# Projecting and norming queries, keys and values by time step in phase one, through DRAM, instead of by tile in phase two

## The chip, the cores and the metric

The kernel runs on one core of a Trainium2 chip. The core has five engines that each work through their own instructions in order: TensorE (PE; its weight loads are listed apart as PEld), VectorE (DVE), ScalarE (ACT), GpSimd (POOL) and SyncE (SP, which here only issues DMAs). They wait for each other through semaphores. The metric is the device time of one execution in microseconds, lower is better. The median of three runs before the change is 867.8 us (867.76 to 870.64).

## The reference, cut to what matters

The input `x` has 128 sequences of 32 time steps with 256 channels; `cond` has one vector of 256 per sequence.

```python
# layer 0: a recurrence over the 32 steps, started at q = p = cond, driven by x
for t in range(32):                                   # RK4: four derivatives a step
    q, p = rk4_step(q, p, x[:, t], coupling, bias)    # tanh(q) @ coupling.T, q**3, ...
    trace[:, t] = q
x = x + mx_ffn(trace, w_gate, w_up, w_down)           # block-quantized gated FFN, 256 -> 1024 -> 256

# layer 1: attention over the 32 steps of each sequence, modulated by cond
scale, shift = split(cond @ W_emb + b_emb)
xn = rms_norm(x, g_norm) * (1 + scale) + shift
q, k, v = split(xn @ W_qkv)                           # 256 -> 768, 16 heads of 16
q, k = rms_norm(q, g_q), rms_norm(k, g_k)             # over the 16 channels of each head
o = softmax(q @ k.T * 16 ** -0.5) @ v
y = o + o @ W_out
# a second FFN: Hadamard rotation, 8-bit activations, ternary weights, 256 -> 1024 -> 256
x = x + h_ffn(y, w1_gate, w1_up, w1_down)
```

Layer 0 walks in time with all 128 sequences in the partitions. The attention of layer 1 needs all 32 steps of a sequence.

## The kernel before

**Phase one** goes by time step: a tile is [128 sequences, 256 channels] of one step. `drive` transposes the step's input, `step` does the recurrence (four slopes, each a chain of tanh on ACT at L594, products with `coupling` on PE at L601, a cube on POOL at L608 and sums on DVE at L552; the new state is written at L645), and `ffn0` does the first FFN of the step: quantizing, DMA transposes (L434), gate and up products (L929), silu (L937), the product on DVE (L941), down products (L976), and the store of the sum to `x1_dram` (L984). `ffn0` ends with the modulated norm: a square sum (L988), an inverse root on POOL (L993, L994), and then gain and shift. For the steps before `T - LATE` the scaling is done on ACT (L999) and gain and shift on POOL (L1003, L1007); for the last `LATE` steps DVE does both (L1012, L1014). The result is transposed on PE (L1015) and copied by ACT (L1017) with a stride of 32 elements into one SBUF tile `xnT` [128, 2, 128 sequences, 32 steps], in which a sequence's steps lie side by side. In the first 78 us the quantizing of the first FFN's weights (`mx_weight`) runs beside the first steps of the recurrence; `ternary_weight` prepares those of the second towards the end of phase one.

**Phase two** (`tokens`) goes by 32 tiles of 128 tokens: 4 sequences with their 32 steps each. The first tile waits for all 32 copies into `xnT`. A tile multiplies its 128 columns of `xnT` with `W_qkv` (`qk` at L1125, `v` at L1132, into PSUM slots of `ps_one`). ACT copies the values into a pad of 17 columns per head whose last column is 1 (L1141) and squares queries and keys (L1142); DVE sums the squares per head (L1143). `rsqrt` takes the inverse root by integer arithmetic on DVE (L1091) and ten tiny instructions on POOL (L1099 to L1109), after one that scales (L1088). DVE then multiplies the queries (L1148) and the keys (L1155) from PSUM with it; the keys go into a zeroed pad (three buffers of `coupling` that phase one no longer needs, cleared at L1052; those for the values are filled at L1058). POOL multiplies the queries with the gains (L1160), DVE transposes queries and keys in 32x32 blocks (L1167, L1169). Small matmuls make the logits (L1177) and the weighted values (L1207); softmax, output rotation (L1230), quantizing, gate and up (L1263), three butterfly stages split over POOL and DVE (L1294), a PE transpose (L526, `turn`), the Hadamard products (L1305), the down products (L1328) and the store (L1338) follow.

**Order.** Nothing runs in the order of the source. Each `add(engine, cost, fn, reads, writes, ..., rank=...)` makes an item; `Work.order` plays a list scheduler with the written costs, forth and back up to 40 times, and keeps the order with the earliest end. Buffers are taken from pools of slots (`states` has 6, `mid` 10); an item that finds none free waits. `port=True` keeps such items of POOL and DVE apart in the plan. `keep_warm` puts matmuls of zeros (L1354) into planned gaps of PE. All items of phase one are issued before those of phase two on every engine, and PSUM is divided anew between them (`ps_gu`, `ps_turn` and others in phase one, `ps_one` and `ps_two` in phase two). All DMAs, transposes too, go through SP's queue.

Of the kernel before, what the change touches and what calls it, by code (L numbers as in the profile page):

```python
# [20 lines left out]
P = 128  # L21
# [12 lines left out]
HEADS = 16  # L34
# [154 lines left out]

# [133 lines left out]
def kernel(  # L323
# [45 lines left out]
    states = slots("states", N, 6)  # L369
# [9 lines left out]
    slim_8 = slots("slim_8", N, 2, FP8)  # L379
    phase_one = ExitStack()  # L380
# [88 lines left out]
    b_xnT, xnT = fixed("xnT", [P, NC, B, T])  # L469
    xnT_flat = xnT.rearrange("p c b t -> p c (b t)")  # L470
    x1_dram = dram.tile([B, T, N], F32, name="x1_dram")
    x1_flat = x1_dram.rearrange("b t d -> (b t) d")
    out_flat = out.rearrange("b t d -> (b t) d")
# [87 lines left out]
    started, xnT_done, x1_stored = [], [], []  # L561
# [317 lines left out]
    LATE = 5  # L879
# [14 lines left out]
    def ffn0(t, q):  # L894
# [115 lines left out]
        else:  # L1010
# [5 lines left out]
        xnT_done.append(  # L1016
            add(ACT, 0.4, lambda: nc.scalar.copy(xnT[:, :, :, t], two(px.ap)), [px], fills=[b_xnT], rank=rank)  # L1017
        )

    q = Buf(())  # L1020
    q.slots, q.slot, q.writers = b_condT.slots, 0, b_condT.writers
    p = b_p
    weights_rank = -300.0
    TERNARY = 24
    parts = ((w0_gate, w0gT, b_w0g), (w0_up, w0uT, b_w0u), (w0_down, w0dT, b_w0d))
    for n, (w, dst, b_dst) in enumerate(parts):
        for part in range(2):
            mx_weight(w, dst, b_dst, part, weights_rank + 2 * n + part)
    modulation(-200.0)
    b_hf, had_ffn, b_qkv, w_qkv_sb = constants_of_phase_two(12.0)  # L1030
    d_next = drive(0, FIRST)
    for t in range(T):
        d = d_next
        if t + 1 < T:
            x_of[t + 1] = load_x(x_step, t + 1, t - 501.0)
            d_next = drive(t + 1, t - 499.9)
        q, p = step(t, q, p, d)
        ffn0(t, q)
    parts = ((w1_gate, w1gT, b_w1g), (w1_up, w1uT, b_w1u), (w1_down, w1dT, b_w1d))
    for n, (w, dst, b_dst) in enumerate(parts):  # L1040
        ternary_weight(w, dst, b_dst, n, T + n, started[TERNARY : TERNARY + 1])


    KPADS, VPADS = 3, 4
    PHASE_TWO = work.SECOND

    k_pads, v_pads = [], []
    pads_ready = []
    for b_c, c_mat in zip(b_coup[:KPADS], coup):
        k_pad = c_mat.rearrange("p c n -> p (c n)").rearrange("p (r a d) -> p r a d", a=4, d=D_HEAD)  # L1050
        pads_ready.append(
            add(POOL, 0.6, lambda k_pad=k_pad: nc.gpsimd.memset(k_pad, 0.0), [], [b_c], rank=float(T))  # L1052
        )
        k_pads.append(Slot(k_pad))

    for i in range(VPADS):
        v_pad = tile_of(f"v_pad{i}", [P, HEADS, D_HEAD + 1])
        nc.gpsimd.memset(v_pad, 1.0)  # L1058
        v_pads.append(Slot(v_pad))

    down_of = []
# [4 lines left out]
    def quantum(name, src, n, cost, rank):  # L1066

        am, sc = Buf(tiny), Buf(tiny)
        add(
            DVE, cost,  # L1070
            lambda: nc.vector.tensor_reduce(  # L1071
                am.ap[:, 0:1], src.ap[:, :n], AX.X, ALU.max, apply_absolute_value=True
            ),
            [src], [am], rank=rank,
        )

        def scales():
            nc.vector.tensor_scalar(am.ap[:, 0:1], am.ap[:, 0:1], EPS_QUANT, 1.0 / 127.0, ALU.max, MULT)
            nc.vector.reciprocal(sc.ap[:, 0:1], am.ap[:, 0:1])  # L1079

        add(DVE, 0.25, scales, [], [am, sc], rank=rank)
        return am, sc
# [30 lines left out]
    def tokens(g):  # L1113
        rank = PHASE_TWO + g
        tok = slice(g * P, (g + 1) * P)
        tt, ts = nc.vector.tensor_tensor, nc.vector.tensor_scalar
        first = list(xnT_done) if g == 0 else []
        behind = down_of[g - 7 : g - 6] if g >= 7 else []


        pqk, pv = Buf(ps_one), Buf(ps_one)

        def qk():
            for c in range(NC):
                nc.tensor.matmul(  # L1125
                    pqk.ap, lhsT=xnT_flat[:, c, tok], rhs=w_qkv_sb[:, c, : 2 * N],
                    start=(c == 0), stop=(c == NC - 1),
                )

        def v():  # L1130
            for c in range(NC):
                nc.tensor.matmul(  # L1132
                    pv.ap[:, :N], lhsT=xnT_flat[:, c, tok], rhs=w_qkv_sb[:, c, 2 * N :],
                    start=(c == 0), stop=(c == NC - 1),
                )

        add(PE, 1.72, qk, [b_xnT, b_qkv], [pqk], rank=rank, after=first, behind=behind)
        add(PE, 0.86, v, [b_xnT, b_qkv], [pv], rank=rank, after=first, behind=behind)
        v_pad, sq, qn, k_pad = Buf(v_pads), Buf(mid), Buf(slim), Buf(k_pads)
        sq_sum, rstd = Buf(tiny), Buf(tiny)  # L1140
        add(ACT, 0.26, lambda: nc.scalar.copy(v_pad.ap[:, :, :D_HEAD], heads(pv.ap[:, :N])), [pv], [v_pad], rank=rank)  # L1141
        add(ACT, 0.477, lambda: nc.scalar.activation(sq.ap, pqk.ap, AF.Square), [pqk], [sq], rank=rank)  # L1142
        add(DVE, 0.6, lambda: nc.vector.tensor_reduce(sq_sum.ap, heads(sq.ap), AX.X, ADD), [sq], [sq_sum], rank=rank)  # L1143

        rsqrt(sq_sum, rstd, 1.0 / D_HEAD, EPS_RMS, rank)
        add(
            DVE, 0.335,
            lambda: tt(heads(qn.ap), heads(pqk.ap)[:, :HEADS, :], spread(rstd.ap[:, :HEADS], D_HEAD), MULT),  # L1148
            [pqk, rstd], [qn], rank=rank,
        )  # L1150

        def k_mult():
            kv = heads(pqk.ap)[:, HEADS:, :].rearrange("p (r e) d -> p r e d", e=2)
            rk = rstd.ap[:, HEADS:].rearrange("p (r e) -> p r e", e=2)
            tt(k_pad.ap[:, :, 0::3, :], kv, rk.unsqueeze(3).to_broadcast([P, PAIRS, 2, D_HEAD]), MULT)  # L1155

        add(DVE, 0.335, k_mult, [pqk, rstd], [k_pad], rank=rank, after=pads_ready)
        add(
            POOL, 0.69,
            lambda: nc.gpsimd.tensor_tensor(  # L1160
                heads(qn.ap), heads(qn.ap), g_prod.unsqueeze(1).to_broadcast([P, HEADS, D_HEAD]), MULT
            ),
            [b_gp], [qn], rank=rank, port=True,
        )

        qT, kT, pl = Buf(slim), Buf(mid), Buf(ps_one)
        add(DVE, 0.335, lambda: nc.vector.transpose(qT.ap, qn.ap), [qn], [qT], rank=rank)  # L1167
        add(
            DVE, 0.63, lambda: nc.vector.transpose(kT.ap, k_pad.ap.rearrange("p r a d -> p (r a d)")),  # L1169
            [k_pad], [kT], rank=rank,  # L1170
        )
# [31 lines left out]
        def attend(group):  # L1203
            for hd in group:
                for j in range(BT):
                    row = slice(j * T, (j + 1) * T)
                    nc.tensor.matmul(  # L1207
                        by_v(po.ap)[row, hd, :], lhsT=by_head(exT.ap)[row, hd, :], rhs=v_pad.ap[row, hd, :],
                        start=True, stop=True,
                    )  # L1210

        for k in range(0, HEADS, HEADS // 2):
            add(
                PE, 0.63, lambda k=k: attend(range(k, k + HEADS // 2)), [exT, v_pad], fills=[po], rank=rank,
# [202 lines left out]
```

## Time and profile before

| | |
|---|---|
| median of 3 runs | 867.8 us |
| the profiled execution | 868.0 us |
| its span | 866.2 us |
| mean granted clock of PE | 0.986 |
| busy in the span: PE, PEld | 795.1 us (92%), 598.6 us (69%) |
| DVE, ACT, POOL | 732.2 us (85%), 494.0 us (57%), 615.9 us (71%) |
| moved by DMA | 55.53 MB, mean 64 GB/s |

The profile is one execution. An engine is busy while an instruction of its own runs; waits, branches and DMA issues are not counted. Matmuls are pipelined and their records overlap, so PE's busy share overstates its work; the distance between starts is the better measure. A line number is a line of the kernel; helpers such as `turn` (L526) and `load` (L444) have one line for many uses, and the names of the tiles tell them apart. "x8" is a count of instructions, and "[0.39 <-POOL slim L608]" is idle time before an instruction and what ended it.

### The profile page before, as it was taken

What the parts mean: (1) busy time and instruction counts of PE and PEld (TensorE: products, weight loads), DVE (VectorE), ACT (ScalarE), POOL (GpSimd) and SP (SyncE); (2) the same over time, 40 slices, a digit from 0 to 9 for tenths busy, and PEclk for the clock granted to TensorE, in tenths of its full rate; (3) what the DMA queues carried; (4) which work ended last, traced back from release to release, by engine and by line L of the source; (5) the groups of instructions that cost most, each with busy time, mean ns of one, the idle gap of its engine ahead of it and who ended that gap; (6) DMA issues with size and microseconds to landing.
All of it is one profiled execution on the core that took longest, in us unless ns stands there. A gap on an engine that the chain in (4) does not pass through costs nothing. (4 is left out here: it accounts for less than half of the span.)

```text
span 866.2 us, 26286 instructions
## 1 busy us (share of the span) xinstructions
PE 795.1 (92%) x10506; PEld 598.6 (69%) x10506; DVE 732.2 (85%) x1863; ACT 494.0 (57%) x1009; POOL 615.9 (71%) x955
## 2 busy tenths in 40 slices
PE   7789999999999999997789999999999999899986
PEld 4566778877788788775456667666667676576765
DVE  6889989999989999998677887778878788887694
ACT  3233465655466665754335667666767555776755
POOL 5698898888768888899574776656685676676320
PEclk9999999999999999999799999999999999999999
DMA  7222232313122242435500113221221221221334
GB/s 241 84 38 53 59 82 59 74 49 83 35 65 68 70 134 56 92 67 110 117 2 15 27 39 65 49 49 32 52 50 48 56 48 42 48 43 46 60 68 86
DMA packets 128891, 55.53 MB, mean 64 GB/s; under 512 B 102144, under 2 KB 127616, under 8 KB 128768
## 3 DMA queue, kind: packets, MB, share of 16 engines
q1 hardware_dynamic: 128768, 53.85, 26.9%
q8 instruction: 82, 1.34, 0.6%
q14 instruction: 41, 0.34, 0.1%
HBM read 21.32 MB, written 8.39 MB: 34 GB/s over the span
## 5 line engine op out<-in xcount | busy, mean ns | idle before, releaser
L1294 POOL TENSOR_TENSOR wide<-wide 128x512 f32<-128x512 f32 x116 | 149.1, 1306 | 68.7 <-DVE wide L1278 33.6
L601 PEld LDWEIGHTS ps_stage<-slim,coup 128*128 128x128 f32 x1024 | 129.3, 192 | 18.1 <-ACT slim L594 10.6
L601 PE MATMUL ps_stage<-slim,coup 128*128 128x128 f32 x1024 | 139.4, 279 | 0.6 <-ACT slim L594 0.3
L608 POOL TENSOR_TENSOR slim<-slim,slim 128x256 f32<-128x256 f32 x96 | 72.4, 755 | 27.7 <-ACT slim L595 23.0
L587 PE MATMUL ps_stage<-slim,eye 128*128 128x256 f32 x256 | 76.6, 392 | 8.1 <-DVE slim L552 7.8
L587 PE MATMUL ps_stage<-drives,eye 128*128 128x256 f32 x256 | 79.2, 392 | 3.3 <-DVE ps_stage L552 2.0
L956 POOL TENSOR_TENSOR mid<-mid,tiny 128x512 f32<-128x512 f32 x64 | 66.2, 1047 | 3.7 <-DVE tiny L678 3.2
L964 POOL TENSOR_TENSOR wide_bf<-mid,tiny 128x512 bf16<-128x512 fp8e4 x64 | 66.5, 1050 | 1.4 <-DVE mid L888 1.1
L594 ACT ACTIVATE slim<-slim 128x256 f32<-128x256 f32 x96 | 39.3, 409 | 47.4 <-DVE slim L552 44.6
L1305 PE MATMUL ps_two<-had_ffn,wide 128*128 128x128 f32 x512 | 63.3, 278 | 1.3 <-DVE wide L1278 1.2
L595 ACT ACTIVATE slim<-slim 128x256 f32<-128x256 f32 x96 | 39.2, 408 | 43.1 <-DVE slim L552 43.0
L1305 PEld LDWEIGHTS ps_two<-had_ffn,wide 128*128 128x128 f32 x512 | 59.9, 192 | 5.4 <-ACT wide L1300 1.9
L1125 PE MATMUL ps_one<-w_qkv_sb,xnT 128*128 128x512 f32 x128 | 60.7, 599 | 0.5 <-DVE mid L1196 0.2
L1313 ACT ACTIVATE wide<-ps_two,magic,tiny 128x1024 f32<-128x1024 f32 x32 | 38.5, 1203 | 39.5 <-DVE tiny L1079 28.0
L587 PEld LDWEIGHTS ps_stage<-slim,eye 128*128 128x128 f32 x256 | 42.0, 190 | 24.0 <-DVE slim L552 16.1
L1294 DVE TENSOR_TENSOR wide<-wide 128x512 f32<-128x512 f32 x76 | 53.3, 727 | 5.9 <-POOL wide L1294 5.9
L1278 DVE SCALAR_TENSOR_TENSOR wide<-ps_two,tiny,mid 128x512 f32<-128x512 f32 x64 | 46.4, 737 | 12.0 <-ACT mid L1271 11.3
L1207 PEld LDWEIGHTS ps_one<-v_pad,mid 32*32 32x32 f32 x4096 | 42.2, 106 | 20.8 <-issue 15.4
L1271 ACT ACTIVATE mid<-ps_two,tiny 128x512 f32<-128x512 f32 x64 | 43.0, 686 | 21.9 <-PE ps_two L1263 21.6
L1207 PE MATMUL ps_one<-v_pad,mid 32*32 32x17 f32 x4096 | 48.0, 181 | 4.5 <-issue 3.0
L587 PEld LDWEIGHTS ps_stage<-drives,eye 128*128 128x128 f32 x256 | 40.3, 193 | 12.3 <-DVE ps_stage L552 7.7
L1263 PEld LDWEIGHTS <-slim_bf 128*128 128x128 bf16 x256 | 24.0, 97 | 34.3 <-issue 8.3
(169 smaller groups left out, 2188.7 us busy)
## 6 DMA issues: line engine op xcount, KB each, us to landing
x_step<-in_x_dram SPq DMA_DIRECT2D x32, 128.0 KB, 2.1
x_add<-in_x_dram SPq DMA_DIRECT2D x32, 128.0 KB, 2.1
x_dram<-slim SPq DMA_DIRECT2D x32, 128.0 KB, 1.9
slim<-x_dram SPq DMA_DIRECT2D x32, 128.0 KB, 2.6
out_dram<-slim SPq DMA_DIRECT2D x32, 128.0 KB, 1.7
raws<-in_L_ffn_w_gate_dram SPq DMA_DIRECT2D x4, 512.0 KB, 4.8
raws<-in_L_ffn_w_up_dram SPq DMA_DIRECT2D x4, 512.0 KB, 6.3
raws<-in_L_ffn_w_down_dram SPq DMA_DIRECT2D x4, 512.0 KB, 4.0
```

What stands on the lines that cost most here:

```text
L587: PE, cost, lambda: nc.tensor.matmul(ps[i].ap, lhsT=eyes[eye], rhs=src.ap, start=False, stop=False),
L594: add(ACT, 0.32, lambda: nc.scalar.activation(th.ap, qi.ap, AF.Tanh), [qi], [th], rank=rank, table="silu")
L601: nc.tensor.matmul(ps[i].ap[:, sl], lhsT=coup[i][:, c, sl], rhs=two(th.ap)[:, c, :], start=False, stop=(c == NC - 1 and m == NC - 1),)
L608: POOL, 0.685, lambda: nc.gpsimd.tensor_tensor(sq.ap, sq.ap, qi.ap, MULT),
L956: lambda it=it, ks=ks: nc.gpsimd.tensor_tensor(blocks(it.ap), blocks(it.ap), spread(binv.ap[:, ks], BLOCK), MULT),
L964: lambda b8=b8, ks=ks, sl=sl: nc.gpsimd.tensor_tensor(blocks(bq.ap[:, sl]), blocks(b8.ap), spread(bscl.ap[:, ks], BLOCK), MULT),
L1125: nc.tensor.matmul(pqk.ap, lhsT=xnT_flat[:, c, tok], rhs=w_qkv_sb[:, c, : 2 * N], start=(c == 0), stop=(c == NC - 1),)
L1207: nc.tensor.matmul(by_v(po.ap)[row, hd, :], lhsT=by_head(exT.ap)[row, hd, :], rhs=v_pad.ap[row, hd, :], start=True, stop=True,)
L1271: lambda pgu=pgu, act=act: nc.scalar.activation(act.ap, pgu.ap[:, :HALF], AF.Silu, scale=sgu.ap[:, 0:1]),
L1278: lambda pgu=pgu, act=act, sl=sl: stt(it.ap[:, sl], pgu.ap[:, HALF:], sgu.ap[:, 1:2], act.ap, MULT, MULT),
L1294: eng.tensor_tensor(dv[:, :, e, :], sv[:, :, 0, :], sv[:, :, 1, :], op)
L1305: nc.tensor.matmul(pfh.ap[:, sl], lhsT=iT.ap[:, sl], rhs=had_ffn, start=True, stop=True)
```

## The change

The projection, the norm of queries and keys and the padding are taken out of the tiles of phase two and put at the end of every time step of phase one, in a function `token` that `ffn0` calls. There the partitions hold sequences. The step's queries, padded keys and padded values make one row of 256 + 512 + 272 = 1040 floats per sequence, which is stored to a DRAM tensor `tok_dram` [128, 32, 1040]. A tile of phase two loads its 128 rows from it into one of six slots; the first such load waits for all 32 stores. The transposed step goes to a small tile by a plain copy, and the large `xnT` is gone. ACT also copies queries and keys from PSUM to SBUF (`raw`), and DVE's two products read that copy. The pads of six slots are preset once. `rsqrt` is the same function, moved up. `LATE` goes from 5 to 14 and `states` from 6 to 8.

```diff
-    states = slots("states", N, 6)
+    states = slots("states", N, 8)
...
+    KEYS, VALUES, TOKEN = N, N + HALF, N + HALF + HEADS * (D_HEAD + 1)
+    toks = slots("tok", TOKEN, 6)
+    xns = slots("xns", N, 8)
...
-    b_xnT, xnT = fixed("xnT", [P, NC, B, T])
-    xnT_flat = xnT.rearrange("p c b t -> p c (b t)")
+    tok_dram = dram.tile([B, T, TOKEN], F32, name="tok_dram")
+    tok_flat = tok_dram.rearrange("b t d -> (b t) d")
...
-    LATE = 5
+    LATE = 14
...
         add(PE, 0.22, lambda: turn(px.ap, xn.ap), [xn], [px], rank=rank)
-        xnT_done.append(
-            add(ACT, 0.4, lambda: nc.scalar.copy(xnT[:, :, :, t], two(px.ap)), [px], fills=[b_xnT], rank=rank)
+        xnT = Buf(xns)
+        add(ACT, 0.26, lambda: nc.scalar.copy(xnT.ap, px.ap), [px], [xnT], rank=rank)
+        token(t, xnT)
+
+    toks_ready = []
+    for slot in toks:
+        def preset(ap=slot.ap):
+            nc.gpsimd.memset(ap[:, KEYS:VALUES], 0.0)
+            nc.gpsimd.memset(ap[:, VALUES:], 1.0)
+        toks_ready.append(add(POOL, 1.05, preset, rank=1.0))
...
+    def token(t, xnT):
+        rank = t + 0.4
+        tt = nc.vector.tensor_tensor
+        pqk, pv, raw, sq, tok = Buf(ps_gu), Buf(ps_turn), Buf(mid), Buf(mid), Buf(toks)
+        sq_sum, rstd = Buf(tiny), Buf(tiny)
...
+        add(PE, 1.72, qk, [xnT, b_qkv], [pqk], rank=rank)
+        add(PE, 0.86, v, [xnT, b_qkv], [pv], rank=rank)
+        add(
+            ACT, 0.26, lambda: nc.scalar.copy(values(tok.ap)[:, :, :D_HEAD], heads(pv.ap)), [pv], fills=[tok],
+            rank=rank, after=toks_ready,
+        )
+        add(ACT, 0.477, lambda: nc.scalar.activation(sq.ap, pqk.ap, AF.Square), [pqk], [sq], rank=rank)
+        add(ACT, 0.477, lambda: nc.scalar.copy(raw.ap, pqk.ap), [pqk], [raw], rank=rank)
+        add(
+            DVE, 0.6, lambda: nc.vector.tensor_reduce(sq_sum.ap, heads(sq.ap), AX.X, ADD), [sq], [sq_sum],
+            rank=rank,
+        )
+        rsqrt(sq_sum, rstd, 1.0 / D_HEAD, EPS_RMS, rank)
...
+        add(
+            DVE, 0.335,
+            lambda: tt(
+                heads(tok.ap[:, :KEYS]), heads(raw.ap)[:, :HEADS, :], spread(rstd.ap[:, :HEADS], D_HEAD), MULT
+            ),
+            [raw, rstd], fills=[tok], rank=rank, port=True, after=toks_ready,
+        )
+        add(DVE, 0.335, k_mult, [raw, rstd], fills=[tok], rank=rank, port=True, after=toks_ready)
+        tok_stored.append(
+            add(SP, 0.45, lambda: nc.sync.dma_start(tok_dram[:, t, :], tok.ap), [tok], rank=rank, tail=4.0)
+        )
...
     def tokens(g):
...
-        add(PE, 1.72, qk, [b_xnT, b_qkv], [pqk], rank=rank, after=first, behind=behind)
-        add(PE, 0.86, v, [b_xnT, b_qkv], [pv], rank=rank, after=first, behind=behind)
...
+        tok = Buf(toks)
+        add(
+            SP, 0.45, lambda: nc.sync.dma_start(tok.ap, tok_flat[rows, :]), fills=[tok], rank=rank, tail=4.0,
+            after=[*tok_stored, *toks_ready], behind=behind,
+        )
+        def gains():
+            q = heads(tok.ap[:, :KEYS])
+            nc.gpsimd.tensor_tensor(q, q, g_prod.unsqueeze(1).to_broadcast([P, HEADS, D_HEAD]), MULT)
+        add(POOL, 0.69, gains, [b_gp], [tok], rank=rank, port=True)
...
+        add(DVE, 0.335, lambda: nc.vector.transpose(qT.ap, tok.ap[:, :KEYS]), [tok], [qT], rank=rank)
+        add(DVE, 0.63, lambda: nc.vector.transpose(kT.ap, tok.ap[:, KEYS:VALUES]), [tok], [kT], rank=rank)
```

## The prediction

> **What bounds the kernel now.** I read the share of busy time first, then busy time by stage, then the order on single engines inside a stage, then the boundary of the phases. The profiled execution took 868.0 us: a span of 866.2 and 1.8 around it; the median of the runs is 867.8, so the sum below, made against 868.0, needs no scaling. About 0.5% (4.3 us) is what a measurement can tell from no change.
>
> Busy time by stage (columns: PE, PEld, DVE, ACT, POOL, each with its instruction count; then the granted clock, DMA share, GB/s). The cuts are at the first product of gate and up (77.6), the end of the last recurrence step (398), the end of the last copy into `xnT` (431) and the first transpose of phase two (439.7):
>
> ```profile
> 77.60:398.00 320.40, 314.13 (x2075) 249.49 (x2076) 302.29 (x859) 183.37 (x522) 274.22 (x362) 1.00 0.30 70
> 398.00:431.00 33.00, 22.26 (x122) 14.61 (x122) 25.81 (x56) 15.02 (x38) 24.15 (x31) 0.79 0.56 124
> 431.00:439.70 8.70, 8.28 (x27) 4.43 (x27) 3.57 (x8) 2.54 (x5) 3.72 (x14) 1.00 0.12 23
> 439.70:500.00 60.30, 53.37 (x1436) 36.23 (x1434) 48.42 (x117) 30.00 (x50) 38.92 (x105) 0.97 0.07 16
> 500.00:830.00 330.00, 307.83 (x6293) 227.45 (x6293) 264.46 (x642) 220.07 (x310) 213.96 (x381) 0.99 0.23 49
> 830.00:866.20 36.20, 26.84 (x212) 21.59 (x212) 24.49 (x49) 17.70 (x18) 2.95 (x2) 1.00 0.35 79
> ```
>
> In the body of phase one PE is busy 98%, DVE 94%, POOL 86%. In the body of phase two PE is busy 93%, DVE 80%, ACT 67%, POOL 65%. Matmul records overlap, so I checked on PE's timeline that 98% means full. Starts follow each other by 0.43 us, which is what two passes of 128x256 f32 take, without a gap:
>
> ```profile
> 208.28 0.60 PE L587 MATMUL ps_stage<-drives,eye 128*128 128x256 f32 x2
> 208.72 0.59 PE L587 MATMUL ps_stage<-slim,eye 128*128 128x256 f32 x2
> 209.15 0.59 PE L929 MATMUL ps_gu<-w0gT,slim_bf 128*128 128x512 bf16 x2
> 209.58 0.59 PE L587 MATMUL ps_stage<-slim,eye 128*128 128x256 f32 x2
> ```
>
> So PE is the bound in both phases, DVE is just behind it in phase one, and only DVE, ACT and POOL have room in phase two.
>
> At the boundary, one chain runs nearly alone:
>
> ```profile
> 430.35 0.59 ACT L1017 COPY xnT<-ps_turn 128x256 f32<-128x256 f32 x1 [3.22 <-PE ps_turn L526]
> 431.32 5.32 PE L1125 MATMUL ps_one<-w_qkv_sb,xnT 128*128 128x512 f32 x12
> 435.21 0.24 POOL L1099 TENSOR_TENSOR tiny<-tiny 128x32 f32<-128x32 f32 x1 [0.30 <-DVE tiny L1091]
> 438.09 0.25 POOL L1109 TENSOR_TENSOR tiny<-tiny,tiny 128x32 f32<-128x32 f32 x1
> 438.79 0.42 DVE L1155 TENSOR_TENSOR coup<-ps_one,tiny 128x256 f32<-128x256 f32 x1
> 439.72 0.70 DVE L1169 STREAM_TRANSPOSE mid<-coup 128x512 f32<-128x512 f32 x1
> ```
>
> **The change, part by part.** 32 tokens' worth of projection and norm move from phase two to phase one; the amount is the same, since there are 32 time steps and 32 tiles.
>
> *PE.* One tile's four passes at L1125 take 1.71 us and its four at L1132 0.86 (consecutive starts at 579.08, 580.79 in the chain that ended last), so 2.57 a tile, 82.2 us in all. Phase one after 77.6 lasts 353.4 us. PE's work there is 314.1 + 22.3 less the fillers of L1354 (0.9 + 6.8): 328.7, and 24.7 stay unfilled, mostly in the drain after the last recurrence step. With the same unfilled time phase one grows by the whole 82. From below: the drain takes half of the unfilled time, +70. From above it is POOL's turn.
>
> *POOL.* A token's inverse root is one instruction at L1088 (0.29) and ten from 435.21 to 438.34 (3.13): 3.42 us, 109.4 in all, while the planner books 0.24 + 2.4. Away go nine steps of gain and shift (0.727 + 0.742 each, 13.2 us; LATE from 5 to 14) and the clearing at L1052 (2.7). The presets of six slots (0.891 + 0.324 by L1052 and L1058, 7.3 us) fit in the 19.6 us that POOL idles before 77.6. POOL's work after 77.6 goes from 298.4 to 391.9. With its present 55 us of idle time that is 446.9 us, +93.5; at its present 84% it is 464, +111. I take PE's +82, because PE's work (410.9) is still the longer, and keep the others for the range.
>
> *DVE.* By distance of starts, L1143 costs 0.58, L1091 0.11, L1148 and L1155 0.34 each: 1.37 a token, 43.8 in all. Nine more steps of L1012 and L1014 (0.39 + 0.35) add 6.7. DVE after 77.6 goes from 328.1 to 378.6, below PE; it costs nothing beyond PE's 82 as long as that covers it. Without that cover its 50.5 us would meet its own 25.3 us of idle time there: 25 to 50 us.
>
> *ACT.* L1141 (0.37) and L1142 (0.59) move; the copy of queries and keys to `raw` is new and priced by L1142, 0.59. Added are 50 us, less 9 x 0.47 at L999 and about 0.24 a step for the plain copy in place of L1017's strided one. ACT goes from 198 to some 236 of 435: covered by PE. If PE's cover were gone ACT would still have 100 us free.
>
> *The two products now read two SBUF tiles* where L1148 and L1155 read one PSUM operand. Nearest rows: L1294 on DVE, two SBUF operands, 727 ns for 128x512, against 680 at L941 with one in PSUM, so 0.05 us longer at twice the size. I take 0.03 each, 64 of them, 2 us on DVE, not on the path; below nothing if the SBUF read is the shorter, as at L1014 (417 against 421 at L1148).
> The Trainium skill, page "SBUF — State Buffer", section "Who interferes with whom", says that a DVE instruction with two SBUF inputs contends with a GpSimd instruction that reads SBUF. If each of the 64 had to wait out half a POOL instruction (0.36 us by L1003), the sum by that rule, an estimate, is 23 us more on DVE and some of it on the path; the L1294 row shows a tenth of that, and the row decides.
>
> *Stores.* Each step adds a store of 128 rows of 4160 bytes, 520 KB, on SP behind DVE's product of the keys. Issue is 0.33 to 0.53 by the loads of 512 KB. Behind it in SP's queue stand the next x load, the x1 store and two DMA transposes a step (1.25 each): SP issues under 4 us in a step of 11, so there is cover. 32 stores are 17 MB; the 512 KB rows land in 4.0 to 6.3 us. Transfers run at 30% DMA share in phase one, and in 300 to 325, where three such loads pass, the transposes land in 2.6 and 3.2 us against 2.3 and 3.1 overall: up to 0.3 us a transposition, hidden in PE's queue. I take 0, up to 10 us for the phase. Phase two reads the 17 MB back at 23% share: also 0, while the loads run ahead over six slots.
>
> *The boundary.* The last token's chain from `xnT` to the products stays. Between the products and the first transpose come a store and a load that wait for every store before them. By the 128 KB rows (1.9 and 2.6, two issues 0.7) that is 5.2 us; by the 512 KB rows (4.0 and 6.3) 11. I take 4.5 + 4.5 + 0.7, less the 0.5 us that lies there now: +9, with all engines waiting. After it gain and transposes follow as before.
>
> *Phase two.* From 439.7 to the end are 426.5 us. PE's work without fillers is 388.0 - 12.4 = 375.6; of the moved 82.2 us 7.4 lay before 439.7, so 74.8 leave, to 300.8. DVE's work goes from 337.4 by 43.8 - 3.6 to 297.2: level with PE. With PE's unfilled time as now (50.9) the gain is 75; two close engines hinder each other, so I take 73. Bounds: 87, if the waits behind POOL's inverse root (17.3 us at L1148, 7.3 at L1155) held PE and half of the 25.7 us of its gaps in the body close; 40, if DVE keeps its 89 us of idle time. States from 6 to 8 and the dropped pads have no price of their own.
>
> Sum: +82 + 9 - 73 = +18: 868 + 18 = **886 us**.
>
> The skill's page "Perfetto Trace Analysis", section "Optimization Strategy", speaks against this forecast: where the most-contended engine changes over time, interleaving the regimes may help. Here the rows say that PE is the longest in both regimes, so PE's part moves from one full stage to another; only by the rule would the result be the first rival's time.
>
> **Rivals.** *The drain is filled and phase two runs freer* (faster): the tokens' products fill half of 398 to 431, the boundary costs 5, phase two gains 87: +70 + 5 - 87 = -12, 856. For it speak the 0.79 clock and 6.8 us of fillers in the drain, and the three PSUM tiles less per tile; against it, that the last token's chain is as long as before. It decides once phase two drops below 435 - 82 = 353 us and phase one grows by less than 75.
> *POOL sets phase one* (slower still): POOL is planned 0.8 us a token too short, every engine behind it waits in order; +100 + 11 - 73 = +38, 906. For: 86% busy already and +93 us. Against: LATE 14 takes 13 back.
> *The move does nothing for phase two*, since DVE is level: +82 + 9 - 55 = +36, 904.
> *No change*: all terms cancel within 4 us.
>
> **Chances.** Forecast 0.45; POOL or DVE 0.23 together; the drain rival 0.23; no change 0.09. Faster 0.23, same 0.09, slower 0.68. The range 857 to 914 reaches from the drain rival's time to a POOL case with phase one at +107; each end leaves out about 1 in 10. The likeliest case alone spans 873 to 898.
>
> **What would show it.** Right: in the body of phase one PE at 97% or more at 13.3 to 14 us a step, POOL near 90%, the last step's end at about 470, first transposes near 531, then 355 us; a gap of 8 to 10 us on all engines after the last store. Wrong: phase one longer by under 70 (then the drain took the work), or POOL without gaps while PE waits for L1109's successor (then POOL is the bound), or phase two above 370 with DVE over 90%, or transposes that land after 4 us and PE waiting for them (then the 34 MB are not hidden).

## The result, and the profile after

The changed kernel takes 924.6 us (median of 4 runs, 923.1 to 925.7) against 868.4; the ratio is 1.0641, 95% interval 1.0615 to 1.0667. The profiled execution has a span of 923.4 us at a mean granted clock of 0.967. The sign was forecast, the size was not: +56 us (57 between the two profiled executions) instead of +18, above the range.

Lines have moved by a few: the state is written at L648, the copy of the transposed step stands at L1020, `qk` and `v` at L1080 and L1087, square and `raw` copy at L1098 and L1099, the sum per head at L1101, the root at L1047 to L1068, the products at L1109 and L1113, the store at L1120, the load at L1177, gains and block transposes at L1183, L1188, L1189, the butterflies at L1312.

Busy time by stage of the changed kernel (PE, PEld, DVE, ACT, POOL, each with its count; granted clock, DMA share, GB/s). The windows answer to those shown of before: first product of gate and up (79.3), end of the last recurrence step (475.4), end of the last copy to `xns` (527.5), end of the last store's issue (542.5; the last key and query product ends at 542.1), first block transpose (558.3):

```profile
79.30:475.40 396.10, 382.04 (x2287) 286.84 (x2286) 347.02 (x939) 206.06 (x577) 315.99 (x582) 1.00 0.30 80
475.40:527.50 52.10, 41.33 (x208) 24.42 (x208) 39.31 (x100) 25.58 (x66) 44.93 (x110) 1.00 0.45 127
527.50:542.50 15.00, 12.10 (x57) 7.64 (x57) 6.76 (x15) 4.32 (x9) 10.14 (x36) 0.90 0.59 194
542.50:558.30 15.80, 5.54 (x28) 4.25 (x29) 10.53 (x18) 3.58 (x5) 2.37 (x2) 0.57 0.86 256
558.30:620.00 61.70, 51.95 (x1834) 38.85 (x1832) 44.10 (x108) 21.64 (x37) 16.50 (x18) 0.78 0.36 103
620.00:880.00 260.00, 234.51 (x5628) 184.44 (x5627) 225.31 (x522) 187.17 (x251) 155.12 (x128) 1.00 0.46 100
880.00:923.40 43.40, 33.60 (x265) 27.23 (x263) 28.62 (x57) 21.76 (x23) 2.57 (x3) 1.00 0.36 81
```

Read the first line against before's 77.6 to 398: PE 96% (was 98), DVE 88 (was 94), POOL 80 (was 86). Every engine got more work in phase one and yet every engine is a smaller share busy. By these shares no engine became fuller than it was; what got longer is looked for between them. The table below sums the whole difference over the boundaries of the stages:

| | before | after | difference | predicted |
|---|---|---|---|---|
| end of the last transposed copy | 431.0 | 527.5 | +96.5 | +82 |
| from there to the last product | 8.3 | 14.6 | +6.3 | 0 |
| last product to first transpose | 0.5 | 16.2 | +15.7 | +9 |
| first transpose to the end | 426.5 | 365.1 | -61.4 | -73 |
| sum | | | +57.1 | +18 |

The timeline at the boundary, where before one chain ran from the copy to the transpose in 9.4 us. SPq lines are DMA issues, the duration that of the whole group, waits included:

```profile
526.84 0.65 ACT L1020 COPY xns<-ps_turn 128x256 f32<-128x256 f32 x2 [5.36 <-PE ps_turn L529]
534.13 1.28 DVE L799 SCALAR_TENSOR_TENSOR wide_bf<-raws,tiny,wide 128x1024 bf16<-128x1024 f32 x1
534.43 1.10 POOL L1061 TENSOR_TENSOR tiny<-tiny,tiny 128x32 f32<-128x32 f32 x1
538.73 3.79 SPq L1120 DMA_DIRECT2D tok_dram<-tok  x2
541.09 0.25 POOL L1068 TENSOR_TENSOR tiny<-tiny,tiny 128x32 f32<-128x32 f32 x1
541.72 0.42 DVE L1109 TENSOR_TENSOR tok<-mid,tiny 128x256 f32<-128x256 f32 x1
547.95 0.34 SPq L447 DMA_DIRECT2D raws<-in_L_ffn_w_down_dram  x1
548.34 3.21 SPq L706 DMA_TRANSPOSE w1uT<-wide_bf  x2
551.65 1.47 SPq L1177 DMA_DIRECT2D tok<-tok_dram  x3
555.47 2.94 DVE L799 SCALAR_TENSOR_TENSOR wide_bf<-raws,tiny,wide 128x1024 bf16<-128x1024 f32 x2
555.93 3.06 POOL L1183 TENSOR_TENSOR tok<-tok,g_prod 128x256 f32<-128x256 f32 x2 [14.59 <-DMA tok<-tok_dram]
558.33 0.43 DVE L1188 STREAM_TRANSPOSE slim<-tok 128x256 f32<-128x256 f32 x1
```

The last tokens come bunched, so their roots of some 3.4 us each stand in a row on POOL (ending at 541.3), which is the +6.3. The last store is issued by 542.5 and landed at 544.8, but SP does not issue the first load until 551.65: weight loads and transposes of the second FFN's preparation stand ahead of it in the queue. The first gain, which waits for that load, starts 4.3 us later; POOL's 14.59 us of idle time at L1183 are this whole gap. The first transpose then comes another 2.4 us later, behind the gain and behind two instructions of the same weight preparation on DVE (L799).

### The profile page after: what moved, and what is told of

It reads as the page before. It is cut to its first block, busy times and chain, and to the rows that moved or that the text cites. A ratio compares the mean times of both kernels' runs of the same rounds, so it can differ in the third digit from the quotient of the medians.

```text
span 923.4 us, 26745 instructions
## 1 busy us (share of the span) xinstructions
PE 820.4 (89%) x10618; PEld 618.0 (67%) x10618; DVE 763.8 (83%) x1881; ACT 492.1 (53%) x1024; POOL 603.8 (65%) x942
## 5 line engine op out<-in xcount | busy, mean ns | idle before, releaser
L1312 POOL TENSOR_TENSOR wide<-wide 128x512 f32<-128x512 f32 x116 | 151.3, 1331 | 83.0 <-DVE wide L1296 39.5
L604 PEld LDWEIGHTS ps_stage<-slim,coup 128*128 128x128 f32 x1024 | 131.7, 195 | 16.8 <-ACT slim L597 6.5
L611 POOL TENSOR_TENSOR slim<-slim,slim 128x256 f32<-128x256 f32 x96 | 71.3, 743 | 33.1 <-ACT slim L598 28.2
L1183 POOL TENSOR_TENSOR tok<-tok,g_prod 128x256 f32<-128x256 f32 x32 | 25.8, 810 | 83.2 <-DMA tok<-tok_dram 67.6
L967 POOL TENSOR_TENSOR wide_bf<-mid,tiny 128x512 bf16<-128x512 fp8e4 x64 | 66.5, 1050 | 1.3 <-DVE mid L891 1.0
L1312 DVE TENSOR_TENSOR wide<-wide 128x512 f32<-128x512 f32 x76 | 63.4, 868 | 1.2 <-POOL wide L1312 1.1
L1080 PE MATMUL ps_gu<-w_qkv_sb,xns 128*128 128x512 f32 x128 | 62.2, 610 | 1.3 <-ACT xns L1020 1.2
L1225 PEld LDWEIGHTS ps_one<-tok,mid 32*32 32x32 f32 x4096 | 45.1, 110 | 23.0 <-issue 18.0
L1225 PE MATMUL ps_one<-tok,mid 32*32 32x17 f32 x4096 | 51.6, 184 | 7.8 <-issue 6.6
L555 DVE SCALAR_TENSOR_TENSOR slim<-ps_stage,slim 128x256 f32<-128x256 f32 x96 | 40.3, 419 | 16.9 <-PE ps_stage L604 7.5
```

Source lines behind the costliest of these rows:

```text
L604: nc.tensor.matmul(ps[i].ap[:, sl], lhsT=coup[i][:, c, sl], rhs=two(th.ap)[:, c, :], start=False, stop=(c == NC - 1 and m == NC - 1),)
L611: POOL, 0.685, lambda: nc.gpsimd.tensor_tensor(sq.ap, sq.ap, qi.ap, MULT),
L967: lambda b8=b8, ks=ks, sl=sl: nc.gpsimd.tensor_tensor(blocks(bq.ap[:, sl]), blocks(b8.ap), spread(bscl.ap[:, ks], BLOCK), MULT),
L1080: nc.tensor.matmul(pqk.ap, lhsT=two(xnT.ap)[:, c, :], rhs=w_qkv_sb[:, c, : 2 * N], start=(c == 0), stop=(c == NC - 1),)
L1225: nc.tensor.matmul(by_v(po.ap)[row, hd, :], lhsT=by_head(exT.ap)[row, hd, :], rhs=values(tok.ap)[row, hd, :], start=True, stop=True,)
L1312: eng.tensor_tensor(dv[:, :, e, :], sv[:, :, 0, :], sv[:, :, 1, :], op)
```

## Experiments

The first runs set three theories against each other: **PE sets both phases** is the prediction's (the tokens cost phase one their 82 us of PE, and what phase two loses is the same); the others are POOL's inverse root and the trip through DRAM. **The in-order chain** was put up after the first results: no engine sets the time alone; the recurrence runs through ACT, PE, POOL and DVE in a fixed order, and each instruction of a token, on whichever engine, delays the link queued behind it. Where "its own order" is said, the planner's costs were left as they were, so that every engine keeps its order of instructions and only durations change.

**Half of the projection, with a new plan.** Half of the input channels are left out of `qk` and `v` in both kernels, and the planner is told half the cost (41 us of PE less).

```diff
-            for c in range(NC):
+            for c in range(1):
...
-        add(PE, 1.72, qk, [xnT, b_qkv], [pqk], rank=rank)
-        add(PE, 0.86, v, [xnT, b_qkv], [pv], rank=rank)
+        add(PE, 0.86, qk, [xnT, b_qkv], [pqk], rank=rank)
+        add(PE, 0.43, v, [xnT, b_qkv], [pv], rank=rank)
```

> The changed kernel with only the first of the two channel chunks in the projections, which leaves out half of them: 41 us of PE less in phase one, and nothing else. Theory PE (PE sets phase one, so each us of it shows): 880 to 892. Theory POOL (the inverse root's ten instructions a token set phase one): 915 to 925. Theory DRAM (store, load and the queue of SP set the extra time): 900 to 915, since only part of PE's share shows.

> The kernel before with the same half of the projections left out, 41 us of PE less in phase two. Theory PE says that PE's time is worth as much in phase two as in phase one: 826 to 836. If DVE or latency sets phase two instead, as the short gain of phase two in the changed kernel (61 us of 75) might say: 840 to 860.

Measured: 902.5 (1.0393, 1.0377 to 1.0409), 22 us less, and 863.9 (0.9949, 0.9935 to 0.9964), 4.7 less. Half of 41 in the one and a ninth in the other; but the new plans also moved phases (the last copy of the kernel before went from 431 to 441 although phase one's work was the same). The gain of the kernel before was also smaller than either theory had it. So a new plan by itself can move a phase by 10 us, and the next runs keep the order.

**The same cut, each kernel in its own order.** Only the first half of the diff.

> The changed kernel with its order of instructions kept as it is, and only the second chunk's matmuls of the projections left out: 41 us of PE less in phase one. If PE sets phase one: 884 to 895. If POOL's root or the stores set it: 912 to 922. The run in which the order was planned anew gave 902.5, so 895 to 908 would say that PE sets part of it.

> The kernel before, its order kept, with the same matmuls left out: 41 us of PE less in phase two. If PE sets phase two as the prediction read it: 827 to 838. If DVE and the waits between engines set it: 850 to 863.

Measured: 918.3 (1.0592, 1.0561 to 1.0623), 6 of 41 us; and 868.8 (0.9994, 0.9970 to 1.0018), nothing of 41, outside both ranges of the expectation. In the changed kernel PE is now idle for 51 us between 79.3 and the last copy (445.7 us less 394.7 busy), at a clock of 1.00 in the body as before, and the last copy ends at 525.1 instead of 527.5. That is no more than executions differ: it ends at 525.5 in a run below that leaves phase one alone (the 8-bit quantizing of phase two). So in this order PE does not set phase one. The windows of the kernel before show where its cut went:

```profile
439.70:500.00 60.30, 50.38 (x1412) 34.75 (x1412) 48.42 (x115) 30.12 (x49) 38.91 (x101) 0.89 0.08 17
500.00:830.00 330.00, 287.04 (x6194) 212.65 (x6194) 263.25 (x638) 217.74 (x309) 212.88 (x380) 0.97 0.23 48
```

PE has 21 us less to do in the second window, DVE, ACT and POOL have what they had, and the granted clock is lower than before (0.89 and 0.97 for 0.97 and 0.99). This cut is therefore less clean than the other: PE's remaining matmuls take a little longer (L1305 283 ns instead of 278, L1177 225 instead of 219), and over the ten executions the time goes from 863.6 us at a clock of 0.978 to 872.0 at 0.960. The lower clock may have taken back some of what the cut saved; no run separates the two. What is shown is that 27 us less of busy PE in the whole span (795.1 to 768.0) saved no time.

**The root as one power instruction.** POOL's ten small instructions, its scaling's partner on DVE and the second constant are replaced by one power with an exponent tile, in both kernels, planned anew.

```diff
-            tt(t.ap, y.ap, y.ap, MULT)
...
-            tt(y.ap, y.ap, u.ap, MULT)
+            ts(v.ap, v.ap, scale, eps, MULT, ADD)
+            tt(y.ap, v.ap, half32, ALU.pow)
```

> The changed kernel with the inverse root done by one POOL power instruction after the scaling, in place of eleven and DVE's integer step: some 2 us of POOL less a token. Theory PE: phase one keeps its length up to its drain, and only the last tokens' chain of 14.6 us shortens: 908 to 920. Theory POOL: 32 times 2 us: 855 to 875.

> The kernel before with the same short inverse root. Theory PE: POOL has 35% of phase two to spare, so 860 to 868, the gain being the waits of DVE behind the root. Theory POOL, were the root's length on the path in phase two as well: 830 to 850.

A miss: 1045.4 (1.2045, 1.2014 to 1.2076) and 1007.6 (1.1600, 1.1581 to 1.1620). The group of the new instruction in the changed kernel (busy us, mean ns):

```profile
L1051 POOL TENSOR_TENSOR tiny<-tiny,half 128x32 f32<-128x32 f32 x32 | 174.7, 5458 | 2.7
```

It takes 5458 ns for 32 columns where one column (L994 before) takes 588 on average and 548 in the median, so the runs say only that 65 us more of POOL (174.7 for 109.4) cost 121 and 139. That is more than one for one, so POOL's work as such does not account for it. The planner was told 1.1 us for two instructions that take over 5, so the order was made for another kernel; how much of the loss that is, no run tells.

**Shorter roots, own order.** The opposite: nine of the ten instructions left out of the changed kernel (92 us of POOL by distance of starts, 67 of busy records).

```diff
-            tt(t.ap, y.ap, y.ap, MULT)
...
-            tt(y.ap, y.ap, u.ap, MULT)
+            tt(y.ap, y.ap, y.ap, MULT)
```

> The changed kernel, its order kept, with one of the ten POOL instructions of the inverse root and nine left out: some 2.9 us of POOL less a token, 92 us in all, and the root itself is left out with them. If POOL sets phase one: 850 to 870. If PE sets it: only the queue of roots at its end shortens, 908 to 920.

Measured: 905.2 (1.0438, 1.0391 to 1.0484), 19 us less, more than the one theory and far less than the other had; the last copy ends at 513.9 instead of 527.5, and from there to the last product it takes 8.0 us instead of 14.6.

**Both cuts, then DVE's, then ACT's, own order.**

> The changed kernel in its own order of instructions, with both cuts at once: nine of the ten small POOL instructions of each token's inverse root left out (92 us of POOL) and half of the projection's matmuls left out (41 us of PE). Alone the first gave -19 us and the second -6. If one engine is full and the other hides behind it, the two together give no more than the larger plus what the next limit allows: 903 to 906. If both lie on the recurrence's own chain, where every engine works in a fixed order and each link waits behind whatever was planned before it, the gains add: 899. If they hide each other (each covers the other's cut), more than the sum: under 890, with the last copy before 500.

Measured: 900.2 (1.0351, 1.0325 to 1.0377), 24.4 less, where the two alone gave 19.4 and 6.3. In time they add, which one full engine hiding another would not do. At the last copy (506.8) PE's half is worth more behind the short roots, 7.1 us, than alone, 2.4: to some part the two had covered each other.

The next cut lets the sum of squares and both products on DVE work on 4 of 16 channels a head (the products of the keys are cut like those of the queries, and the presets fill whole slots):

```diff
-nc.vector.tensor_reduce(sq_sum.ap, heads(sq.ap), AX.X, ADD)
+nc.vector.tensor_reduce(sq_sum.ap, heads(sq.ap)[:, :, :4], AX.X, ADD)
...
-                heads(tok.ap[:, :KEYS]), heads(raw.ap)[:, :HEADS, :], spread(rstd.ap[:, :HEADS], D_HEAD), MULT
+                heads(tok.ap[:, :KEYS])[:, :, :4], heads(raw.ap)[:, :HEADS, :4], spread(rstd.ap[:, :HEADS], D_HEAD)[:, :, :4], MULT
```

> The changed kernel in its own order of instructions, with three cuts at once: nine of ten small POOL instructions of each token's root left out, half of the projection's matmuls left out, and the three wide DVE instructions of a token work on 4 of 16 channels a head (about 1 us of DVE a token, 32 us; the presets clear whole slots). The first two cuts together gave 900.2. If the tokens' work as such sets phase one, the last copy falls from 506 to 445 or so and the time to 840 to 850. If every engine counts for a part (the in-order chain of the recurrence waits on whichever queue is behind), DVE's 32 us are worth a fifth to a third: 890 to 894. If what holds the time is the order alone, nothing: 898 to 901.

Measured: 885.6 (1.0176, 1.0134 to 1.0218), another 14.6 for 26 us of busy records less on DVE (762.1 to 735.8). The last copy ends at 493.4. Per us of work, DVE counts most of the three, though the prediction had its 50 us covered at no cost. It was cut only with the other two already short, so what it is worth alone is not known. For ACT, the square and the two copies of a token get the same 4 of 16 channels.

> The three cuts of a token on PE, POOL and DVE, in the changed kernel's own order (885.6 together), and ACT's too: the square and the two copies of a token work on 4 of 16 channels a head, about 0.9 us of ACT a token less, 30 us. If ACT lies on the chain like the others, -5 to -10: 876 to 881. If it was covered, as the prediction has it, within 2 of 885.6. What then remains above 868 is not a token's work.

Measured: 885.2 (1.0191, 1.0160 to 1.0223), no difference. ACT was covered, as predicted.

**All four cuts with a new plan.** The planner is told the small costs.

> The same cuts as the run before it, with the planner told the smaller costs, so that the order is planned anew. If the fixed order holds what is left of phase one (last copy 493 with three cuts, 430 before the change), the new order gives it back: last copy 440 to 450, time 825 to 845. If the remaining chain of a token itself or nine more steps of gain and shift on DVE hold it, the last copy stays at 480 to 490 and the time at 870 to 885.

Measured: 863.4 (0.9938, 0.9914 to 0.9963), 22 us less for the order alone. The result lies between the two theories of the expectation: the last copy ends at 478.2. From the last copy to the first transpose its window shows the DMA engines busy throughout, at a share of 1.01:

```profile
478.20:493.10 14.90, 10.36 (x65) 7.52 (x65) 6.09 (x15) 2.93 (x8) 1.83 (x4) 0.89 1.01 306
```

Against 431 before, 47 us of phase one remain, and the part of a token that is left is 41 us of PE. That fits PE as the floor of phase one when nothing else is in its way, but neither the other half of the projection nor the nine more steps of gain and shift on DVE were taken out, so this is not shown.

**The boundary: wait, traffic, weight preparation.** First, the tile loads read the first step's rows, so that none waits for the last stores (own order). Then only 64 of the 1040 columns are stored and loaded (own order). Then the second FFN's weights are prepared from ten steps earlier (new plan).

```diff
-            SP, 0.45, lambda: nc.sync.dma_start(tok.ap, tok_flat[rows, :]), fills=[tok], rank=rank, tail=4.0,
+            SP, 0.45, lambda: nc.sync.dma_start(tok.ap, tok_dram[:, 0, :]), fills=[tok], rank=rank, tail=4.0,
```

> The changed kernel, its order kept, with every tile's load reading the rows of step 0 (the attention is then over wrong tokens): the first loads no longer wait for the last stores, the bytes are the same. If the round trip through DRAM holds the boundary: 914 to 917. If the loads wait in the queue of SP behind the last weights of the second FFN, which come late: 921 to 925.

```diff
-            add(SP, 0.45, lambda: nc.sync.dma_start(tok_dram[:, t, :], tok.ap), [tok], rank=rank, tail=4.0)
+            add(SP, 0.45, lambda: nc.sync.dma_start(tok_dram[:, t, :64], tok.ap[:, :64]), [tok], rank=rank, tail=4.0)
```

The load is cut in the same way.

> The changed kernel in its own order, but each token stores and loads only 64 of its 1040 columns: 32 MB less through DRAM, the same number of DMAs and waits. If the traffic costs (the transposes land later, loads come late): -10 us or more, spread over both phases. If only waits and order count: -2 to -4, at the boundary, where the store and the load land sooner.

```diff
-    TERNARY = 24
+    TERNARY = 14
...
-        ternary_weight(w, dst, b_dst, n, T + n, started[TERNARY : TERNARY + 1])
+        ternary_weight(w, dst, b_dst, n, T - 10 + n, started[TERNARY : TERNARY + 1])
```

> The changed kernel with the second FFN's weights prepared from ten steps earlier, planned anew. If the late weight work at 539 to 558 holds the boundary (it stands in the queue ahead of the first loads of tokens), the gap between the last key product and the first transpose falls from 16 to 6 or 8 us and the time by 8 to 10: 915. If the store, the load and the wait for all stores hold it, it stays at 12 to 16 us and the time within 4 us. A new plan by itself has moved phases by up to 10 us in both directions.

Measured: without the wait 921.8 (1.0613, 1.0580 to 1.0645), 3 less. The first transpose comes at 538.3 instead of 558.3, the second at 542.96, but the third only at 559.31. DVE's timeline of that run in between:

```profile
542.96 0.43 DVE L1188 STREAM_TRANSPOSE slim<-tok 128x256 f32<-128x256 f32 x1
547.67 2.47 DVE L799 SCALAR_TENSOR_TENSOR wide_bf<-raws,tiny,wide 128x1024 bf16<-128x1024 f32 x2
553.77 0.16 DVE L772 TENSOR_TENSOR tiny<-tiny 128x1 f32<-128x1 f32 x1 [3.62 <-ACT wide L766]
556.44 2.95 DVE L799 SCALAR_TENSOR_TENSOR wide_bf<-raws,tiny,wide 128x1024 bf16<-128x1024 f32 x2
559.31 0.43 DVE L1188 STREAM_TRANSPOSE slim<-tok 128x256 f32<-128x256 f32 x1
```

Taking the wait away lets two tiles in and then meets the late weights, here on DVE (L799 and L772). With few bytes it is 915.9 (1.0528, 1.0492 to 1.0565), 8.8 less: the last copy ends at 526.7 as before, the gap from product to transpose is 8 us instead of 16.2, phase two takes 362.2. So the traffic costs phase one no more than executions differ, as predicted, and the boundary 8, which was not. With early weights it is 916.5 (1.0547, 1.0511 to 1.0583), 8.1 less: the gap is 7.0, phase two 353.3, but phase one's last copy ends 12 us later. At the boundary that work had lain beside idle engines; put earlier, it lies in the busy phase one. How much of the 12 us that is, and how much the new plan, was not separated.

**Phase two, own order.** Nine of ten root instructions left out in the kernel before (the diff above); and the abs-max of the two 8-bit quantizings reads a quarter of the channels, in both kernels.

```diff
-                am.ap[:, 0:1], src.ap[:, :n], AX.X, ALU.max, apply_absolute_value=True
+                am.ap[:, 0:1], src.ap[:, : n // 4], AX.X, ALU.max, apply_absolute_value=True
```

> The kernel before in its own order, nine of the ten small POOL instructions of each tile's root left out (92 us of POOL in phase two). Half of the projection taken from PE there gave 0. If POOL's root sets phase two before the change (DVE's products wait 17 and 7 us for it), -20 to -30: 840 to 848, and that is what moving it takes away. If DVE sets it, or the chain of a tile with its ten buffers, -5 or less: 863 to 868.

> The kernel before in its own order, the abs-max of the two 8-bit quantizings of phase two reads a quarter of the channels (about 1.2 us of DVE a tile, 38 us in all). If DVE sets phase two, -25 or more: under 843. If no engine alone does, a fifth to a third as POOL's cut gave in the changed kernel: 856 to 861. If POOL or the order, within 3 of 868.

> The changed kernel in its own order with the same cut on DVE in phase two (about 1.2 us a tile, 38 us). If DVE, which the prediction has level with PE at 297 and 301 us in phase two after, is the limit there, -20 or more: under 905. If PE is, within 4 of 924.6. If it is a chain through all engines, 912 to 918.

Measured: 854.9 (0.9830, 0.9789 to 0.9871), 14.4 less for POOL's 92 us; 862.2 (0.9918, 0.9890 to 0.9946), 7.2 less for 27 us of DVE's records; 916.2 (1.0531, 1.0494 to 1.0569), 8.4 less for 29 us (of which 2 lie ahead of the last copy, where nothing was cut). All three lie between nothing and the whole, as the chain theory says, which named no closer number. The 38 us of DVE in the expectations were too many: the shorter instruction saved 27 and 29.

**A version 1.5% faster than the kernel before.** The experiments point to POOL's root in phase two of the kernel before. Its first refinement is left out; by the start's error of 3.4% the second one alone leaves about 1e-4.

```diff
-            tt(t.ap, y.ap, y.ap, MULT)
-            tt(t.ap, t.ap, v.ap, MULT)
-            ts(t.ap, t.ap, -0.5, 1.5, MULT, ADD)
-            tt(y.ap, y.ap, t.ap, MULT)
-
```

> The kernel before in its own order, the inverse root of a tile in six POOL instructions instead of ten (the first of two refinements left out; the second, of higher order, leaves a relative error of about 1e-4, worked out from the start's 3.4%). 40 us of POOL less in phase two, where 92 us gave 14.4: -6.3 by that price, 862 to 864. If only the last few instructions were covered: -10 or more; if the first: within 2 of the kernel before.

Measured: 856.1 (0.9850, 0.9826 to 0.9875), 13 us less for 40 by distance of starts. That is nearly all that 92 us gave: once the root is 1.3 us a tile shorter, the rest of it is covered. The waits of DVE from 500 to 830, first before, then with the short root (engine, line, what it waited for: us in total, times, longest):

```profile
DVE slim L1148 <- POOL tiny L1109: 13.7, 13, 2.7
DVE coup L1155 <- POOL tiny L1109: 7.3, 7, 1.6
DVE tiny L1143 <- ACT mid L1142: 7.4, 9, 1.4
```

```profile
DVE slim L1143 <- POOL tiny L1104: 3.4, 4, 1.4
DVE coup L1150 <- POOL tiny L1104: 0.4, 1, 0.4
DVE tiny L1138 <- ACT mid L1137: 9.8, 12, 1.7
```

The products' waits for POOL fall from 21.0 to 3.8 us; the wait of the sum for ACT's square grows by 2.4. Against the 17 us less in these waits, the time falls by 13.

## Why the prediction was right in sign and wrong in size

**The step that failed** is "So PE is the bound in both phases", as a reading of busy shares, and with it the rule by which all the sums were made: take the longest engine's work, and book the others' at nothing "as long as that covers it". Four lines of PE's timeline without a gap were taken as proof that 98% busy is full; they covered under 2 us, and that PE has no gap in a stretch does not show that less work on PE would bring the end nearer. Cuts in the kernels' own order show what each engine's work is worth:

| engine's work cut | size, us | time saved, us |
|---|---|---|
| PE, phase one after | 41 (31 of records) | 6 |
| POOL, phase one after | 92 (67 of records) | 19 |
| DVE, phase one after, with the two above | 26 | 15 |
| ACT, with the three above | 23 | 0 |
| PE, phase two before | 41 (27 of records) | 0, at a lower clock |
| POOL, phase two before | 92 (70 of records) | 14 |
| DVE, phase two before | 27 | 7 |

A kernel in which PE sets the time would have 41 in the first row and the fifth. All this holds for the two orders as they are: with a new plan the first cut was worth 22.

**Phase one**, +96.5 for +82 (1.7 of it ahead of the first gate product, 75.7 in the body, 19.1 in the drain after the last step). The tokens' work on POOL and DVE was priced as hidden under PE. It isn't: with POOL's roots short the last copy ends 13.6 us earlier, with PE's half too 20.7, with DVE's 34.1. The term of 82 itself may be near the floor, by the re-planned run with all cuts, but that is not separated. The rival "POOL sets phase one" had +100 and so the size nearest to the result, which is luck: its root, all but taken out, gives back 13.6 us and not 96, and POOL is 80% busy. One part of that rival stays open: the planner books a root at 2.64 us where it takes 3.42, and no run told it the real price.

**The products with two SBUF operands.** Their groups before (the kernel before, 439.7 to 830) and after (79.3 to 542), with mean ns after the busy us:

```profile
L1148 DVE TENSOR_TENSOR slim<-ps_one,tiny 128x256 f32<-128x256 f32 x31 | 13.1, 421 | 17.3 <-POOL tiny L1109 17.0
L1155 DVE TENSOR_TENSOR coup<-ps_one,tiny 128x256 f32<-128x256 f32 x31 | 12.8, 414 | 7.3 <-POOL tiny L1109 7.3
```

```profile
L1113 DVE TENSOR_TENSOR tok<-mid,tiny 128x256 f32<-128x256 f32 x32 | 17.3, 542 | 14.3 <-POOL tiny L1068 13.9
L1109 DVE TENSOR_TENSOR tok<-mid,tiny 128x256 f32<-128x256 f32 x32 | 15.5, 484 | 0.0
```

They cost 191 ns a token more, 6.1 us in all, against 2 by the row that the prediction took. The medians are as before (422 and 418). The difference is 11 of the 64 that take 647 to 1262 ns, and each of the 11 started while POOL was in a multiplication of two SBUF tiles, L611 or L967, as here:

```profile
139.06 0.73 POOL L611 TENSOR_TENSOR slim<-slim,slim 128x256 f32<-128x256 f32 x1
139.14 0.94 DVE L1113 TENSOR_TENSOR tok<-mid,tiny 128x256 f32<-128x256 f32 x1 [2.03 <-POOL tiny L1068]
```

Before, with one operand in PSUM, 36 of the 64 started in the same way while POOL was in an instruction on two SBUF tiles of over 500 ns (L1160, L1294), and none took more than 426 ns. So the direction of the Trainium skill's rule in "SBUF — State Buffer", section "Who interferes with whom", is seen here, at a quarter of the 23 us that the estimate by it gave, because few of the products meet one for long.

In phase two the butterflies on DVE, also with two SBUF operands, went from 727 to 868 ns on average, 76 of them, 10.7 us. Their rows before and after (min, median, max):

```profile
L1294 DVE TENSOR_TENSOR wide<-wide x76: 629/681/1360, 480.6 to 848.7; 128x512 f32<-128x512 f32 x76
L1312 DVE TENSOR_TENSOR wide<-wide x76: 628/684/1782, 612.3 to 906.7; 128x512 f32<-128x512 f32 x76
```

The medians are equal. 7 of the 76 were longer than 760 ns before and 20 after, and all 27 started beside POOL's own butterflies or its gain. So the new order lays more of them side by side. It also shows a misreading in the prediction: the 727 ns of L1294, "0.05 us longer" than L941, were a mean over a few such meetings; the median, 681, is L941's 680. The row that was to decide the price held no price for the operand, only the rate of meetings in another order.

**The boundary**, +22 for +9. The store and the load cost less than the 4.5 each that were booked: 2.6 for the last store, 4.3 from the first load's issue to the gain. What was not in the sum is what stands around them: the roots of the last tokens in a row on POOL (6.3), 6.8 us from the last store's landing to the first load's issue with the second FFN's weights ahead in SP's queue, under transfers at 256 GB/s, and 2.4 us of gain and weight work before the first transpose. Fewer bytes and earlier weights each halve the gap. The prediction looked at the queue behind the store during phase one, but not at what is queued there between the last store and the first load.

**Phase two**, -61.4 for -73. PE's work was sized well: without fillers it is 301.9 us (predicted 300.8). But it was not what had set the time, so no 75 us of it could be booked one for one. How the 61 us divide among the engines was not measured; the root alone gave 14 when it was cut there. Two things stand against the gain in the trace, neither priced by a run: the butterflies' 10.7 us, and a start at a granted clock of 0.78 for 62 us (0.97 before) after the idle boundary. The named signs read as follows: PE at 97% or more in the body of phase one (96%), last step's end about 470 (475.4), first transposes near 531 (558.3), then 355 us (365.1), POOL near 90% (80%).

**What held.** ACT costs nothing; the stores cost phase one nothing that shows; the amount of PE's work that moves; and that the sum of the terms is a loss. The rival on the other side needed the drain to take half of its unfilled time. The drain after the last step grew instead, from 33.0 to 52.1 us, at 79% PE. The section "Optimization Strategy" of the skill's "Perfetto Trace Analysis", which spoke for that rival, finds no support in these runs: moving work between the two regimes cost 56 us.

## What to carry to other kernels

In a kernel of in-order queues with three engines 80% busy or more, don't price a move by the longest engine's work and the rest at nothing: cut one engine's work at a time with the order kept, and use what each cut is worth (here 0 to 0.55 us a us). A full-looking engine is shown to be the bound only when work taken from it shortens the time. Before a mean is taken as a price, look at the median and the longest: a few meetings with another engine can make the whole difference. And for a new trip through DRAM read the issuing queue from the last store to the first load, not only the two transfers.

## What the runs showed of the hardware, unexpected

POOL's power instruction with an exponent tile takes 5458 ns for 128x32, where 128x1 took 588 before (median 548). The granted clock fell when half of the projection was taken out of the kernel before (0.960 to 0.978 over ten executions, for 0.980 to 0.994) and the time stayed; within those ten a lower clock went with a longer time, so which of the two follows the other is open. In the changed kernel the same cut left the clock where it was (0.956 to 0.969 for 0.963 to 0.967). DVE's products of two SBUF tiles took up to 1262 ns instead of some 420 when they started beside a POOL multiplication of two SBUF tiles; with one operand in PSUM none of 36 meetings with such an instruction of POOL took more than 426. And at 534.43 a POOL instruction that takes 0.25 us elsewhere took 1.10, ending 0.12 us after DVE's L799 of 1.28 beside it, an instruction with two SBUF operands: one case in which POOL's small one was held up, and not the reverse.
